# A graph layer with 27 instead of 35 ranges summed through slots, and the other nodes by row gathers

## The chip, the cores and the metric

The kernel runs on one core of one Trainium2 chip. The metric is the device time of one execution in microseconds; the time of a kernel is the median of its runs. TensorE multiplies matrices and writes to PSUM, VectorE (DVE in the profile) and ScalarE (ACT) compute on SBUF and PSUM, GpSimd (POOL) issues the gathers, and SyncE (SP) issues most of the plain transfers. Each engine works through its own queue in order.

## The reference

A graph has 6250 nodes with 128 features each and 100000 edges (src, dst, type), sorted by dst. Every edge sends the source's row, multiplied by one of two weight matrices, to its destination; the messages are summed per destination, the node's own product is added, and a ReLU, a residual and a layer norm follow.

```python
Xs = X[src]
m_data = Xs @ W_data.T + b_data
m_ctrl = Xs @ W_control.T + b_control
msg = jnp.where((edge_types == 0)[:, None], m_data, m_ctrl)
agg = jax.ops.segment_sum(msg, dst, num_segments=X.shape[0])
out = agg + (X @ W_self.T + b_self)
x = _layernorm(x + jax.nn.relu(out), axis=-1)
```

## The kernel before

**The message table.** For 49 blocks of 128 nodes both products with bias are made (line 448 and 450), split into three bf16 parts whose sum is the float32 value, and kept in SBUF as `m3` (98 tiles of 128 rows by 384 columns: a block and a type each). The same goes to DRAM as `table` (line 479), from which rows can be gathered. `brows` holds the three bf16 parts of the bias as rows, and the product with `one3` (line 450) adds it; the parts are made on VectorE (lines 399 to 408).

**Ranges with slots.** The first 35 x 160 = 5600 nodes are 35 ranges of `WN` = 160 destinations, in groups of 1, 2 and eight times 4. The edges of a range (at most 21 x 128) are loaded as `win`. `ranks` (from line 589) numbers the edges of each of the 98 tiles of `m3`: for each of 21 steps VectorE makes a mask of the tile numbers (`hots`, line 645), TensorE counts with it in PSUM (`rk`, line 655), and VectorE reads the count off with a maximum (`slot`, line 659). An edge thus has a tile and a slot, 32 per tile. Masks `hr` and `two` (674, 680) and the product `vt` (689) put each edge's row and destination into its slot; the rows go to DRAM as `packed` and come back to all partitions as `rows` (line 840, 784 KB for a range). Edges without a slot go into a list of up to 64 per range (`hl`, line 756), whose rows are gathered from `table` in pairs of ranges (`sr`, line 797, index `at`, line 785).

`sums` then works through the 25 groups of four tiles of each range. VectorE turns `rows` into a mask (line 847) and makes the mask of destinations `hot2` (line 854). TensorE picks the rows out (`g`, line 867), ScalarE writes them to SBUF as `gs` (line 413), and TensorE adds them to the destinations (`a`, lines 881 and 884).

**Gathered nodes.** The last 650 nodes are six blocks of up to 128 (`gathered`, from line 899). A block has up to 18 tiles of 128 edges. For each tile GpSimd issues a gather of 128 rows of `table`, 768 bytes each (`t_msg`, line 931, four buffers), VectorE makes a mask of destinations (`t_hot`, line 936, three buffers), and TensorE adds the rows to `ga` (line 942). That is 93 tiles.

**Closing.** `close` adds the three parts on VectorE (line 530), adds the residual, and normalises (lines 538 to 576), for the ranges of a group or for a gathered block. `counts` collects how many edges were summed; if they aren't all, a slower path would run, which isn't the case here.

**The order.** All operations are recorded with a cost and a due time, and `Plan.run` puts them into one order: for each engine the operation that can start first, the earliest due first. The engines' queues, and which of ScalarE and VectorE takes a copy, come from this list. `T0` and `TW` are the due time of the first range and the step from range to range in this plan; `gathered` spreads its tiles evenly from `g0` to `g1`. A wait between engines costs the plan `SEM`; a transfer's time is its `lat`. A buffer that is used again makes its next user wait for all users of the one before.

Of the kernel before, what the change touches and what calls it, by code (L numbers as in the profile page):

```python
# [10 lines left out]
F32 = mybir.dt.float32  # L11
BF16 = mybir.dt.bfloat16
I32 = mybir.dt.int32
AF = mybir.ActivationFunctionType
ALU = mybir.AluOpType
AX = mybir.AxisListType
SP = mybir.EngineType.SP
# [4 lines left out]
P = 128  # L22
D = 128
D3 = 3 * D
# [9 lines left out]
WIN = KT * P  # L34
GROUPS = [1, 2] + [4] * 8
NW = sum(GROUPS)
# [194 lines left out]
def sums_over_windows(ctx, tc, x, xt, edges, w, bias, out, total):  # L231
# [16 lines left out]
    def C(shape, dtype, name):  # L248
        return Buf(plan, const, shape, dtype, name, 1)

    T0 = 46.0
    TW = 13.0
# [5 lines left out]
        r0.t, edges.rearrange("(p h k) c -> p h (k c)", p=125, h=RH)[:, :, 1:2]), 0.0, w=[r0],  # L258
        lat=2.0)
    w_sb = C([D, D3], F32, "w_sb")  # L260
    b3 = C([3, D3], F32, "b3")
    add("ACT", 0.1, lambda: A.dma_start(w_sb.t, w), 0.0, [], [w_sb], lat=2.5)
    add("ACT", 0.1, lambda: A.dma_start(b3.t, bias.to_broadcast([3, D3])), 0.0, [], [b3], lat=2.5)

# [7 lines left out]
    def vec(due, cols, fn, r, w, rate=1.04):  # L272
        return add("DVE", dve(cols, rate), fn, due, r, w)
# [68 lines left out]
    def count_rows():  # L342
# [13 lines left out]
        in_offset=bass.IndirectOffsetOnAxis(ap=row_i.t[:, 0:1], axis=0)),  # L356
        0.5, [row_i], [er], lat=2.5)
    dst_f = C([NBD, RL], F32, "dst_f")
# [19 lines left out]
    def load_edges(b, n, out_, due, buf, key, engine):  # L378
        def fn():
# [6 lines left out]
            else:  # L386
# [4 lines left out]

    part = C([3, D3], BF16, "part")
    left = C([3, D3], F32, "left")
    acc3 = C([3, D3], F32, "acc3")
    part2 = C([3, D3], BF16, "part2")
    brows = C([P, D3], BF16, "brows")
    bd = 2.0
    vec(1, D3, lambda: V.memset(brows.t, 0.0), [], [brows], 0.3)
    vec(bd, D3, lambda: V.tensor_copy(part.t, b3.t), [b3], [part])
    vec(bd, D3, lambda: V.tensor_scalar_mul(acc3.t, part.t, ident.t[:3, 0:1]),  # L400
        [part, ident], [acc3])
    vec(bd, D3, lambda: V.tensor_sub(left.t, b3.t, part.t), [b3, part], [left])
    vec(bd, D3, lambda: V.tensor_copy(part2.t, left.t), [left], [part2])
    vec(bd, D3, lambda: V.scalar_tensor_tensor(acc3.t, part2.t, ident.t[:3, 1:2], acc3.t,
                                               op0=ALU.mult, op1=ALU.add),
        [part2, ident, acc3], [acc3])
    vec(bd, D3, lambda: V.tensor_sub(left.t, left.t, part2.t), [part2, left], [left])
    vec(bd, D3, lambda: V.scalar_tensor_tensor(brows.t[:3, :], left.t, ident.t[:3, 2:3], acc3.t,
                                               op0=ALU.mult, op1=ALU.add),
        [left, ident, acc3], [brows])  # L410

# [18 lines left out]
    for q in range(NS):  # L430
# [12 lines left out]

        def products(bs=bs, c=c, xa=xa, mp=mp, q=q):
            for i, b in enumerate(bs):
                o = mp.t[:, 256 * i : 256 * i + 256]
                at = (b - c * CH) * P
                T.matmul(o, xa.t[:, at : at + P], w_sb.t[:, : 2 * D], start=i == 0, stop=False,  # L448
                         skip_group_check=True)
                T.matmul(o, one3.t, brows.t[:, : 2 * D], start=False, stop=q < DQ,  # L450
                         skip_group_check=True)
        add("PE", 0.55 * nb, products, due, [xa, w_sb, one3, brows], [mp])
        ts = slice(4 * q, 4 * q + 2 * nb)
# [445 lines left out]
    def gathered(bi, when, step):  # L899
# [28 lines left out]
        for k in range(nt):  # L928
            at = when + step * k
            m = B(work, [P, D3], BF16, "t_msg", 4)  # L930
            add("POOL", 1.25, lambda m=m, k=k: G.indirect_dma_start(  # L931
                out=m.t, out_offset=None, in_=table[:, :],
                in_offset=bass.IndirectOffsetOnAxis(ap=idx.t[:, k : k + 1], axis=0)),
                at, [idx, table_b], [m], lat=2.0)
            hot = B(work, [P, P], BF16, "t_hot", 3)
            vec(at + 2, P, lambda hot=hot, k=k: V.tensor_scalar(
                hot.t, iota1_b.t[:, :P], code.t[:, k : k + 1], None, op0=ALU.is_equal),
                [code, (iota1_b, 0)], [hot], 0.26)

            def mm(m=m, hot=hot, k=k):  # L940
                for j in range(-(-nn // R)):
                    T.matmul(ga.t[R * j : R * j + R, :D3], hot.t[:, R * j : R * j + R], m.t,  # L942
                             start=k == 0, stop=False, skip_group_check=True)
            add("PE", 0.165, mm, at + 4.5, [hot, m], [ga])
# [8 lines left out]
    for gi, nw in enumerate(GROUPS):  # L953
        if gi == 0:
            when, step, engines = 4.0, 0.5, ["SP"]
        elif gi == 1:
            when, step, engines = 19.0, 0.9, ["SP", "ACT"]
        else:
            when, step, engines = T0 + w0 * TW - 58, 1.8, ["SP"]
            if gi == 2:  # L960
                when, step = 40.0, 1.3
        todo.append((gi, w0, nw, when, step, engines))
        w0 += nw
# [8 lines left out]
    total_tiles = sum(GT)  # L972
    g0, g1 = T0 + 2.5 * TW, T0 + (NW - 2.5) * TW
    done = 0
# [151 lines left out]
```

## Time and profile before

| what | us |
|---|---|
| median of 3 runs | 669.11 (669.08 to 672.03) |
| profiled execution | 620.9 |
| its span, first to last instruction | 619.1 |
| VectorE: counts of line 659, 128x392, 168 times | 93.7 |
| VectorE: masks of line 854, 175 times | 93.6 |
| VectorE: masks of line 847, 70 times | 43.0 |
| ScalarE: `gs`, 836 times | 353.8 |
| TensorE: `g`, line 867, 3430 times | 316.8 |
| TensorE: `a`, line 881, 3360 times | 306.0 |
| TensorE: `ga`, line 942, 363 times | 39.0 |
| GpSimd: `t_msg`, 93 times | 95.5 |

The times per group are busy times; products of TensorE that run beside each other on different columns of the array overlap, so the rows of TensorE add up to more than its busy time. In the same way an instruction of VectorE can begin before the one ahead of it has ended. The profiled execution is shorter than the median of the runs; comparisons within the profile use its own time.

The transfers, by their queue, are packets, megabytes and share of the 16 engines' time:

```profile
q1 hardware_dynamic: 45585, 48.25, 24.3%
q0 software_dynamic: 5664, 10.97, 6.7%
q10 hardware_dynamic: 7494, 6.53, 3.4%
```

Queue 0 is GpSimd's, with 93 row gathers, 18 list gathers and one of edges; queue 1 is SP's and queue 10 ScalarE's.

### The profile page before, as it was taken

Reading aid. Unit: us, or ns where it says so; the run is one execution under the profiler, and the core shown is the slowest. Engines: PE = TensorE matmul, PEld = TensorE weight load, DVE = VectorE, ACT = ScalarE, POOL = GpSimd, SP = SyncE. Lnnn points to the kernel's source line nnn. Section 1 sums busy time; section 2 is a strip of 40 time slices with the busy share of each in tenths; the row PEclk is TensorE's granted clock in tenths of the full one; section 3 lists DMA queues with packets and bytes.
Section 4 is the critical chain, followed back from the end, with each engine's and each line's share of the span. In section 5 each row is a group of like instructions: output and inputs, shape, how many; then the busy total and the mean of one; then the engine's idle time right before and its main releaser. Section 6 shows DMA issues by size and latency. Waiting matters only on the chain.

```text
span 619.1 us, 31669 instructions
## 1 busy us (share of the span) xinstructions
PE 540.9 (87%) x13418; PEld 415.5 (67%) x13418; DVE 521.1 (84%) x1846; ACT 445.7 (72%) x1153; POOL 115.1 (19%) x119
## 2 busy tenths in 40 slices
PE   3899959979998898989979998998899889998991
PEld 2555637757776677767767877777777678776670
DVE  4899789989999899988998999899988987866602
ACT  1477736757677767867867788778777777788991
POOL 1000230020421034310134410045100333110000
PEclk9999988989999999999999999999999999999997
DMA  4688651063135223540344143315420443043001
GB/s 113 194 269 266 196 178 38 25 207 104 44 103 153 84 65 100 177 127 5 118 141 140 51 134 99 101 50 168 133 85 4 156 122 109 24 139 105 27 4 28
DMA packets 58893, 67.85 MB, mean 110 GB/s; under 512 B 19707, under 2 KB 49906, under 8 KB 58743
## 3 DMA queue, kind: packets, MB, share of 16 engines
q1 hardware_dynamic: 45585, 48.25, 24.3%
q0 software_dynamic: 5664, 10.97, 6.7%
q10 hardware_dynamic: 7494, 6.53, 3.4%
q8 instruction: 107, 1.75, 1.1%
q14 instruction: 43, 0.35, 0.2%
HBM read 50.72 MB, written 13.27 MB: 103 GB/s over the span
## 4 chain that ended last, share of the span: by engine, by line
DVE 55%; PE 30%; ACT 5%; DMA 4%; issue 4%; SPq 1%; POOL 0%; ACTq 0%; DVEq 0%
DVE hot L854 10%; DVE slot L659 9%; PE a L881 9%; PE g L867 8%; DVE hots L645 4%; PE rk L655 4%; DVE rows L847 4%; DVE two L680 4%; ACT gs L413 3%; PE g L448 3%; DVE s L530 3%; DVE st L542 2%; DVE hr L674 2%; DVE xr L538 2%; PE a L884 2%
## 5 line engine op out<-in xcount | busy, mean ns | idle before, releaser
L413 ACT CAST gs<-g 128x384 bf16<-128x384 f32 x836 | 353.8, 481 | 93.5 <-PE g L867 88.6
L867 PE MATMUL g<-m,rows 128*32 128x384 bf16 x3430 | 316.8, 329 | 1.9 <-issue 1.1
L881 PE MATMUL a<-gs,hot 128*32 128x384 bf16 x3360 | 306.0, 331 | 9.1 <-ACT gs L413 5.1
L867 PEld LDWEIGHTS <-rows 128*32 128x32 bf16 x3430 | 217.4, 135 | 14.6 <-issue 2.1
L884 PE MATMUL a<-gs,hot 128*32 128x128 bf16 x2520 | 200.9, 220 | 0.1
L881 PEld LDWEIGHTS <-hot 128*32 128x32 bf16 x3500 | 153.4, 95 | 62.8 <-issue 27.0
L931 POOL DMA_INDIRECT t_msg<-table,t_idx x93 | 95.5, 1027 | 243.3 <-PE ga L942 196.9
L659 DVE TENSOR_REDUCE slot<-rk 128x4 f32<-128x392 f32 (+2 forms) x210 | 106.6, 507 | 18.2 <-PE rk L655 15.5
L854 DVE TENSOR_TENSOR hot<-iota_b,to_d 128x800 bf16<-128x800 bf16 x175 | 93.6, 565 | 21.0 <-PE a L884 16.6
L884 PEld LDWEIGHTS <-hot 128*32 128x32 bf16 x2625 | 98.0, 96 | 4.7 <-issue 0.3
L655 PE MATMUL rk<-hots,rest 128*32 128x392 bf16 (+2 forms) x800 | 73.2, 317 | 25.9 <-DVE slot L659 25.2
L655 PE MATMUL rk<-hots,tri 128*32 128x392 bf16 (+2 forms) x840 | 82.7, 314 | 0.0
L655 PEld LDWEIGHTS <-rest 128*32 128x32 bf16 x800 | 34.9, 96 | 48.4 <-issue 43.6
L645 DVE TENSOR_TENSOR hots<-iota_b,st 128x392 bf16<-128x392 bf16 (+2 forms) x210 | 60.1, 327 | 1.8 <-PE vt L689 1.6
L797 POOL DMA_INDIRECT sr<-table,at x18 | 17.1, 949 | 183.4 <-DVE at L785 99.9
L847 DVE TENSOR_SCALAR rows<-rows,pid 128x1568 bf16<-128x1568 bf16 x70 | 43.0, 635 | 0.0
L942 PE MATMUL ga<-t_msg,t_hot 128*32 128x384 bf16 x363 | 39.0, 326 | 2.7 <-DVE s L530 2.2
L655 PEld LDWEIGHTS <-tri 128*32 128x32 bf16 x840 | 36.3, 97 | 3.5 <-issue 0.3
L530 DVE TENSOR_TENSOR s<-s,a 128x128 f32<-128x128 f32 x70 | 19.8, 284 | 18.0 <-ACT s L527 16.8
L448 PE MATMUL g<-w_sb,xc 128*128 128x256 f32 x98 | 32.8, 430 | 1.3 <-PE rk L655 0.9
L689 PEld LDWEIGHTS <-two 128*64 128x64 bf16 x735 | 18.6, 108 | 16.7 <-DVE two L680 13.7
L689 PE MATMUL vt<-hots,two 128*64 128x98 bf16 x735 | 24.1, 208 | 6.0 <-DVE two L680 5.7
(174 smaller groups left out, 568.7 us busy)
## 6 DMA issues: line engine op xcount, KB each, us to landing
rows<-packed SPq DMA_DIRECT2D x35, 784.0 KB
table<-m SPq DMA_DIRECT2D x12, 384.0 KB
table<-m ACTq DMA_DIRECT2D x12, 384.0 KB
xc<-in_xt SPq DMA_DIRECT2D x8, 320.0 KB
xr<-in_x SPq DMA_DIRECT2D x8, 256.0 KB
out<-xr SPq DMA_DIRECT2D x8, 256.0 KB
gl<-sr SPq DMA_DIRECT2D x35, 48.0 KB
xc<-in_xt ACTq DMA_DIRECT2D x6, 256.0 KB
```

The source lines that it names most:

```text
L413: [("ACT", act(cols), lambda: A.copy(o(), src())), ("DVE", dve(cols), lambda: V.tensor_copy(o(), src()))], None, None, due, r, w, lat)
L448: T.matmul(o, xa.t[:, at : at + P], w_sb.t[:, : 2 * D], start=i == 0, stop=False, skip_group_check=True)
L645: vec(due - (2.0 if k else 0.5), nw * NT, lambda k=k, hot=hot, k0=k0: V.tensor_tensor(hot.t[:, k - k0].rearrange("p w (c d) -> p w c d", d=2),
L655: T.matmul(acc.t[R * j : R * j + R, : nw * NT], wt.t[:, R * j : R * j + R], m, start=start, stop=stop, skip_group_check=True)
L659: vec(due, nw * NT, lambda k=k: V.tensor_reduce(slot.t[:, k, :], acc.t[:, : nw * NT].rearrange("p (w c) -> p w c", c=NT), axis=AX.X, op=AL ...
L689: T.matmul(vv()[q : q + 64, i // 2, :], two.t[:, (k - k0) * nw + i].rearrange("p f r -> p (f r)"), hot.t[:, k - k0, i, :], start=k == 0 an ...
L847: add("DVE", dve(half * NT, 0.26), lambda sp=sp, rs=rs: V.tensor_scalar(sp.t[:, rs], sp.t[:, rs], pid1.t, None, op0=ALU.is_equal), due - 4 ...
L854: V.tensor_tensor(hot2.t[:, c0 : c0 + 5].rearrange("p g (c d) -> p g c d", d=2), iota1_b.t.rearrange("p (c d) -> p c d", d=2)[:, None].to_ ...
L867: T.matmul(gp.t[R * t : R * t + R, :D3], sp.t[:, :, 4 * g + t], m3.t[:, 4 * g + t, :], start=True, stop=True)
L881: T.matmul(a.t[R * j : R * j + R, :D3], hot2.t[:, g, R * j : R * j + R], gs.t, start=g == 0, stop=False, skip_group_check=True)
L884: T.matmul(a.t[R * c : R * c + R, D3:], hot2.t[:, g, P:], gs.t[:, c * D : (c + 1) * D], start=False, stop=last, skip_group_check=True)
L931: add("POOL", 1.25, lambda m=m, k=k: G.indirect_dma_start(out=m.t, out_offset=None, in_=table[:, :], in_offset=bass.IndirectOffsetOnAxis(a ...
```

## The change

Two of the eight groups of four ranges go: 27 ranges (4320 nodes) are summed through slots, and the last 1930 nodes are 16 blocks with 273 gathers. Gathered rows have eight buffers instead of four, their masks four instead of three. The bias is split on ScalarE and VectorE as one row, and its three parts are put into `brows` by three transfers. The plan gets other due times and other costs: the first range is due at 36 instead of 46, the first two groups' ranking has its own starts and steps, the loads of `r0` and `er` are costed longer, and the products of the message table are planned one block at a time instead of two. Gathers are spread from two ranges after the first to two before the last, instead of two and a half. From about line 410 on, a line of the kernel after stands seven lines above its place before.

```diff
-GROUPS = [1, 2] + [4] * 8
+GROUPS = [1, 2] + [4] * 6
...
-    T0 = 46.0
+    T0 = 36.0
...
-        lat=2.0)
+        lat=4.5)
...
-    b3 = C([3, D3], F32, "b3")
+    b1 = C([1, D3], F32, "b1")
...
-        0.5, [row_i], [er], lat=2.5)
+        0.5, [row_i], [er], lat=6.5)
...
-    vec(bd, D3, lambda: V.tensor_copy(part.t, b3.t), [b3], [part])
-    vec(bd, D3, lambda: V.tensor_scalar_mul(acc3.t, part.t, ident.t[:3, 0:1]),
-        [part, ident], [acc3])
...
+    vec(0.2, D3, lambda: V.memset(brows.t, 0.0), [], [brows], 0.3)
+    add("ACT", 0.4, lambda: A.copy(bparts[0].t, b1.t), 1, [b1], [bparts[0]])
+    vec(1, D3, lambda: V.tensor_sub(left.t, b1.t, bparts[0].t), [b1, bparts[0]], [left])
+    add("ACT", 0.4, lambda: A.copy(bparts[1].t, left.t), 1, [left], [bparts[1]])
+    vec(1, D3, lambda: V.tensor_sub(bparts[2].t, left.t, bparts[1].t), [left, bparts[1]],
+        [bparts[2]])
+    for i in range(3):
+        add("SP", 0.1, lambda i=i: S.dma_start(brows.t[i : i + 1, :], bparts[i].t), 1.5,
+            [bparts[i]], [(brows, i)], lat=2.0)
...
-        def products(bs=bs, c=c, xa=xa, mp=mp, q=q):
-            for i, b in enumerate(bs):
+        for i, b in enumerate(bs):
+            def product(i=i, b=b, c=c, xa=xa, mp=mp, q=q):
...
-        add("PE", 0.55 * nb, products, due, [xa, w_sb, one3, brows], [mp])
+            add("PE", 0.58, product, due, [xa, w_sb, one3, brows], [mp])
...
-            m = B(work, [P, D3], BF16, "t_msg", 4)
+            m = B(work, [P, D3], BF16, "t_msg", 8)
...
-            hot = B(work, [P, P], BF16, "t_hot", 3)
+            hot = B(work, [P, P], BF16, "t_hot", 4)
...
-            when, step, engines = 4.0, 0.5, ["SP"]
+            when, step, engines = 3.0, 0.9, ["SP"]
         elif gi == 1:
-            when, step, engines = 19.0, 0.9, ["SP", "ACT"]
+            when, step, engines = 18.0, 1.1, ["SP", "ACT"]
         else:
             when, step, engines = T0 + w0 * TW - 58, 1.8, ["SP"]
             if gi == 2:
-                when, step = 40.0, 1.3
+                when, step = 36.0, 1.3
...
-    g0, g1 = T0 + 2.5 * TW, T0 + (NW - 2.5) * TW
+    g0, g1 = T0 + 2 * TW, T0 + (NW - 2) * TW
```

More of the change, by code (lines that the diff above doesn't have):

```diff
@@ L258, in sums_over_windows @@
         r0.t, edges.rearrange("(p h k) c -> p h (k c)", p=125, h=RH)[:, :, 1:2]), 0.0, w=[r0],
-        lat=2.0)
+        lat=4.5)
     w_sb = C([D, D3], F32, "w_sb")
-    b3 = C([3, D3], F32, "b3")
+    b1 = C([1, D3], F32, "b1")
     add("ACT", 0.1, lambda: A.dma_start(w_sb.t, w), 0.0, [], [w_sb], lat=2.5)
-    add("ACT", 0.1, lambda: A.dma_start(b3.t, bias.to_broadcast([3, D3])), 0.0, [], [b3], lat=2.5)
+    add("ACT", 0.1, lambda: A.dma_start(b1.t, bias), 0.0, [], [b1], lat=2.5)
     iota_f = C([P, P], F32, "iota_f")
@@ L389, in load_edges @@
         add(engine, 1.0 if b else 0.1, fn, due, [first] if b else [], [(buf, key)], lat=2.0)
[L392 to L395, printed above, removed]
+    left = C([1, D3], F32, "left")
+    bparts = [C([1, D3], BF16, f"bpart{i}") for i in range(3)]
     brows = C([P, D3], BF16, "brows")
-    bd = 2.0
-    vec(1, D3, lambda: V.memset(brows.t, 0.0), [], [brows], 0.3)
-    vec(bd, D3, lambda: V.tensor_copy(part.t, b3.t), [b3], [part])
-    vec(bd, D3, lambda: V.tensor_scalar_mul(acc3.t, part.t, ident.t[:3, 0:1]),
-        [part, ident], [acc3])
[L402 to L410, printed above, removed]
+    vec(0.2, D3, lambda: V.memset(brows.t, 0.0), [], [brows], 0.3)
[7 more added lines that the diff above has]
+            [bparts[i]], [(brows, i)], lat=2.0)
     evict = lambda o, src, cols, due, r, w, lat=0.0: add(
```

## The prediction, made before the run

> **What bounds the kernel now.** I read the page's busy shares first, then the slices, then the chain of waits for landmarks, then a table of stretches, then GpSimd's own timeline.
>
> ```profile
> span 619.1 us, 31669 instructions
> PE 540.9 (87%) x13418; PEld 415.5 (67%) x13418; DVE 521.1 (84%) x1846; ACT 445.7 (72%) x1153; POOL 115.1 (19%) x119
> DVE  4899789989999899988998999899988987866602
> DVE 55%; PE 30%; ACT 5%; DMA 4%; issue 4%; SPq 1%; POOL 0%; ACTq 0%; DVEq 0%
> ```
>
> VectorE and TensorE are both near full, and VectorE carries 55% of the chain that ends last. Its row of slices is at 8 to 9 until the last tenth of the span and then falls: three regimes. The chain shows where they meet, because each group of four ranges builds one list (`hl`, line 756) at the end of its ranking:
>
> ```profile
> 126.58 0.96 DVE hl L756
> ...
> 244.12 0.97 DVE hl L756
> ...
> 483.00 0.96 DVE hl L756
> 544.01 0.56 PE vt L775 x24
> ```
>
> Columns: start, length, what. The third group's list is at 126.6; from 244.1 to 483.0 four groups pass, 59.7 us each; the last group's list is at 544, and 75 us of ranges without any ranking follow. In stretches:
>
> ```profile
> core 0: us, PE busy (x) PEld busy (x) DVE busy (x) ACT busy (x) POOL busy (x), PEclk, DMA share, GB/s
> 220.00:500.00 280.00, 256.89 (x6939) 205.53 (x6933) 257.39 (x878) 214.96 (x568) 70.06 (x69) 1.00 0.34 103
> 545.00:605.00 60.00, 54.69 (x1457) 41.71 (x1451) 28.07 (x94) 53.44 (x143) 1.90 (x2) 1.00 0.20 69
> ```
>
> In the middle VectorE is busy 257.4/280 = 92%, so 54.9 us per group; TensorE shows the same 92%. At the end VectorE is at 47% and TensorE and ScalarE lead. GpSimd has 70 us of work in 280.
>
> **What the Trainium skill says.** "Perfetto Trace Analysis", section "Identifying the Most-Contended Engine": occupancy is a fair measure for VectorE, matmul occupancy isn't, because matmuls are pipelined, and weight-load share is better. Here weight loads are 205.5/280 = 73%, so I take VectorE as the bound of the middle and TensorE's 92% as overstated. The same page, "DMA Instruction — SWDGE (GPSIMD)": the profiler ends a gather when its descriptors are written, not when the data is there. The trace agrees: the first row gather takes 0.96 us on GpSimd, yet TensorE waits until 4.74 us after its start. "SBUF — State Buffer", section "SBUF: two separate sides": a VectorE instruction in a two-port fast mode and GpSimd's descriptor writing lock each other out. The trace shows at most a mild form:
>
> ```profile
> L931 POOL DMA_INDIRECT t_msg<-table,t_idx x93: 940/946/2396, 74.4 to 528.1; - x93
> ...
> L936 DVE TENSOR_SCALAR t_hot<-iota_b,t_code x93: 235/247/487, 44.5 to 529.7; 128x128 bf16<-128x128 bf16 x93
> ```
>
> Minimum, median, maximum in ns: half of the gathers are within 6 ns of the fastest although VectorE is 92% busy around them.
>
> **The change, part by part.**
>
> *Eight ranges leave (two groups of four).* Count times mean over the VectorE rows of the groups table gives about 616 us against 521 busy, since neighbours overlap a little: I scale sums by 521/616 = 0.85. With the instruction counts of both programs' issue order: ranking falls from 316 to 248, slot and hot masks (lines 847, 854) from 143 to 111, closing from 72 to 56, small copies by 3, the bias by 3: 121 less, 103 scaled. ScalarE's evictions fall from 836 to 647 of the 128x384 kind, 189 x 0.48 = 91 us by the mean. TensorE: a unit of one `g` and one `a` product takes 0.37 to 0.41 us where TensorE streams (534 matmuls, 11 to a unit, in the stretch 580 to 600), so eight ranges of 25 are 80 us, with their ranking about 100.
>
> *180 more row gathers (93 to 273), ten more blocks (6 to 16).* VectorE pays one `t_hot` a gather, 0.258 us, and per block: two adds 0.55, relu-add 0.29, statistics 0.29 and 0.18, seven small operations 1.1, half of the normalising 0.2, nine list instructions 1.48: 4.1 us, or 0.23 per gather at about 17.5 gathers. So 180 x 0.49 = 88, scaled 75. TensorE: four matmuls of 384 columns, side by side, 0.165 us a gather where they stream: 30 us, and 5 for ten blocks' own product. ScalarE: 10 us.
>
> Net: VectorE 521 - 103 + 75 = 493, priced instruction by instruction 577 x 0.85 = 488. TensorE loses about 65, ScalarE about 80. So the time saved is far from eight ranges' 2 x 59.7 = 119.
>
> *Where it falls.* Counting gather matmuls between one range's products and the next in the issue order: before, 42 gathers in the four groups of the middle, 10.5 a group; after, 223 in ranges 2 to 21, 44.6 a group, and 42 more in the ranges after the last ranking. A group after: 54.9 + 34.1 x 0.49 x 0.85 = 69.1 us of VectorE. TensorE and ScalarE now have slack (TensorE 256.9/280 x 59.7 = 54.8, and 34 x 0.165 + 1 more: 61; ScalarE 45.8 and 2 more: 48), so VectorE's share should rise from 92% to 94 or 95%: 73 us. The ends: at 92%, 75; at 97%, 71.
>
> *GpSimd's pace.* Gathers can't follow each other faster than this:
>
> ```profile
> 224.72 0.95 POOL L931 DMA_INDIRECT t_msg<-table,t_idx  x1 [0.30 <-issue]
> 225.97 0.95 POOL L931 DMA_INDIRECT t_msg<-table,t_idx  x1 [0.30 <-PE ga L942]
> ```
>
> 1.25 us each with 0.30 between. A group needs 44.6 + 2 for its long lists (line 797): 58 us of 73. It fits with 20% to spare, but GpSimd's queue is in order: a list gather that waits for VectorE's `at` (line 785; 99.9 us of such waits before, in eight waits) holds all row gathers behind it, and TensorE, in order too, then stops at a `ga` product. Eight buffers instead of four are what covers this: at one product per 1.6 us they hold 13 us. I cost it at 1 us a group inside the 73; from below it is nothing, and if the cover is gone, 5 to 10 a group. Row gathers move 98 KB each, and queue 0 took 6.7% of the engines for 111: 287 would be about 19%, beside 20 to 25% of the rest. No bound.
>
> *Buffers and loads.* Four `t_hot` instead of three, and the separate product of each block with its own issue slot: nothing. Ten more loads of edges, rows and results on SP: 0.4 us of issue each, behind which nothing is late; at worst 4 us.
>
> *The start.* The bias leaves VectorE (eight instructions, 3.4 us, until 10.25) for a chain of ScalarE and VectorE copies and three transfers. In SP's queue these stand behind some 20 loads, whose issues ended at 11.2 before, so `brows` comes at about 13 to 14, not 10.25. Ahead of it TensorE does the first range's ranking, which started at 10.3 and can now start at 4 to 5, when its edges have landed. VectorE has 107 us of work in the first 127 either way. I take 4 us gained, between 10 gained and 4 lost.
>
> *The end.* Five ranges without ranking follow as before, but now with 42 gathers: TensorE, near full there, pays 42 x 0.165 + 1.4 = 8 us, plus a block to close: 9 (5 to 20).
>
> **Sum.** 122.6 + 5 x 73 - 5 (the first such group took 54.7 where the others took 60) + 75.2 + 9 = 567 us of span against 619.1. The profiled execution as a whole took 620.9, the median of the runs shown is 669.11, so 48 us lie outside what this profile explains. If they scale (a slower clock outside the profiler would do that; no row shows it), 669.11 x 567/619.1 = 613; if they are fixed, 617. VectorE-bound work scales less than TensorE's with TensorE's clock, which pulls down. I take 613.
>
> **Rivals.** (a) *Gathers set the pace without undoing the gain:* TensorE stops at `ga` products and groups take 79 to 83 us. For it: in-order queues, 80% use of GpSimd. Against: 0.5 us of such waits in the whole profile before. Span 597, so 645. (b) *Slower:* one mechanism, the cycle of a gather (buffer free, issue, landing, product) is stretched by VectorE's lock on the port and by the broadcast `rows` transfers. It decides when a cycle exceeds 83.5/46.6 = 1.79 us: 122.6 + 5 x 84 - 5 + 75.2 + 9 = 622, already above 619.1, or 672. For it: the 2.4 us maximum; against: the median. (c) *Faster than forecast:* the 48 us are TensorE's clock, and the lighter TensorE gets most of it back: the 567 us then carry some 25, so 592. (d) *The sums cancel:* VectorE's 488 to 493 plus more stops leave it at 619.
>
> **How the numbers follow.** Forecast 0.62 (595 to 632 alone), (a) 0.16, (b) 0.10, (c) 0.09, (d) 0.03. Below half a per cent a difference can't be told in this kernel. Faster 0.62 + 0.16 + 0.09 = 0.87, same 0.03, slower 0.10. The range takes in most of (a) and (c): 588 to 648.
>
> **What would show it.** Right: lists (line 749 after) 70 to 76 us apart, VectorE over 92% busy between them, GpSimd at 70 to 80% of its pace, almost no wait of TensorE or GpSimd on a landing, span 550 to 585. Wrong: TensorE idle before `ga` on a DMA or VectorE waiting for `t_hot` buffers (a, b); gathers with a median far over 0.95 us (b); a start later than 127; the timed median not following the span.

## The result, and the profile after

The changed kernel takes 703.86 us (median of 4 runs, 700.36 to 706.68) beside 669.13 for the kernel before (669.08 to 672.03): ratio 1.0498, 95% interval [1.0466, 1.053]. It is slower; the forecast was 613 us. Its page:

```profile
span 698.7 us, 27684 instructions
...
PE 533.3 (76%) x11386; PEld 369.0 (53%) x11386; DVE 490.3 (70%) x1905; ACT 375.5 (54%) x953; POOL 294.2 (42%) x295
...
DVE  5798368987877378878588775977866768664432
...
PE 56%; DVE 9%; ACT 9%; issue 9%; another core or an unknown queue 6%; DMA 1%; ACTq 0%; DVEq 0%; SPq 0%
```

The work is what was forecast: VectorE's 490.3 us lie inside the 488 to 493 of the prediction. But VectorE is now busy 70% of the span instead of 84%, its slices stand at 7 and 8, and it carries 9% of the chain instead of 55%. No engine is full. So the time is in waits. The waits by engine and line (total us, how often, the longest):

```profile
PEld L874 <- issue: 156.5, 227, 5.2
ACT gs L406 <- PE g L860: 125.9, 167, 9.2
...
PE a L874 <- ACT gs L406: 59.9, 80, 5.2
ACT gs L406 <- remote: 52.7, 15, 7.5
```

All are on the path `g` product, eviction `gs`, `a` product. None of them names a gather, and in the whole list no engine waits for the landing of gathered rows: that is not what is late. "issue" is time for which the profile shows no reason, "remote" a releaser that it doesn't show. One stop, in the timeline (start, length, what, idle time before and its releaser):

```profile
230.33 0.95 POOL L924 DMA_INDIRECT t_msg<-table,t_idx  x1 [0.30 <-issue]
...
231.58 0.95 POOL L924 DMA_INDIRECT t_msg<-table,t_idx  x1 [0.30 <-issue]
...
231.68 0.48 PE L860 MATMUL g<-m,rows 128*32 128x384 bf16 x1 [0.34 <-issue]
...
232.40 0.10 PEld L874 LDWEIGHTS <-hot 128*32 128x32 bf16 x1 [1.29 <-issue]
...
232.83 0.95 POOL L924 DMA_INDIRECT t_msg<-table,t_idx  x1 [0.30 <-issue]
...
234.08 0.94 POOL L924 DMA_INDIRECT t_msg<-table,t_idx  x1 [0.30 <-issue]
...
236.80 1.24 ACT L406 CAST gs<-g 128x384 bf16<-128x384 f32 x3 [7.52 <-remote]
...
237.33 0.51 PE L874 MATMUL a<-gs,hot 128*32 128x384 bf16 x4 [5.17 <-ACT gs L406]
```

GpSimd writes one gather after another from 225.1 to 235.0. The last `g` product starts at 231.68; ScalarE, idle, evicts at 236.80, and then three evictions at once. TensorE's wait is put down to ScalarE, but ScalarE only sat there. What came late is TensorE's report that the products were done: the trace records no step of TensorE's semaphore (the counter on which the other engines wait) between 229.47 and 236.72, then three within 0.23 us (worked out from the trace, in which some 2% of these records are missing). The ends of matmuls in these profiles are modelled, so a product that ended late can't be told from a signal that left late; below, "TensorE's signals are late" means either. The stretch with the stop, and the one behind it (columns as in the table of stretches above: start and end, length, busy us of each engine, TensorE's granted clock, share of the transfers, GB/s):

```profile
225.00:246.00 21.00, 12.31 (x220) 8.16 (x210) 9.67 (x37) 7.19 (x19) 10.05 (x10) 0.76 0.36 114
246.00:254.00 8.00, 6.61 (x183) 5.13 (x182) 6.70 (x23) 5.66 (x17) 3.15 (x3) 1.00 0.55 181
```

The clock is 0.76 over this stretch and back at 1.00 after it. The Trainium skill, "TensorE: Matmul & The Clock Gate", section "HAM oscillation — how this bites in real kernels", says that gaps of over about 3.4 us without matmuls make the clock fall. In this trace less is enough: the clock is recorded at half from 231.6 to 241.8, so its fall comes as the 5 us stop begins, not after it, and in the 3.4 us before each of the trace's eleven falls 8 to 51 matmuls started, with no pause between starts over 2.7 us (worked out from the trace; where work streams, as in e7 below, 3.4 us hold about 79). Over the whole span the clock is 0.932, against 0.982 in the profile before.

One number in all this can't be understood without the next: the profiled execution of the kernel before took 620.9 us, all its timed runs here 669. The experiments show that these are two conditions, and that the prediction was worked out in the one and measured in the other.

### The profile page after: what moved, and what is told of

It is laid out like the page before. It is cut to its first block, busy times and chain, and to the rows that moved or that the text cites. A ratio compares the mean times of both kernels' runs of the same rounds, so it can differ in the third digit from the quotient of the medians.

```text
span 698.7 us, 27684 instructions
## 1 busy us (share of the span) xinstructions
PE 533.3 (76%) x11386; PEld 369.0 (53%) x11386; DVE 490.3 (70%) x1905; ACT 375.5 (54%) x953; POOL 294.2 (42%) x295
## 4 chain that ended last, share of the span: by engine, by line
PE 56%; DVE 9%; ACT 9%; issue 9%; another core or an unknown queue 6%; DMA 1%; ACTq 0%; DVEq 0%; SPq 0%
PE a L874 18%; PE g L860 17%; PE ga L935 8%; ACT gs L406 8%; PE rk L648 5%; PE a L877 3%; PE vt L682 2%; DVE slot L652 2%; DMA rows<-packed 1%; DVE rows L840 1%; DVE s L523 1%; PE a L480 1%; DVE two L673 1%; DVE hot L847 1%
## 5 line engine op out<-in xcount | busy, mean ns | idle before, releaser
L406 ACT CAST gs<-g 128x384 bf16<-128x384 f32 x647 | 284.4, 482 | 251.3 <-PE g L860 125.9
L924 POOL DMA_INDIRECT t_msg<-table,t_idx x273 | 278.1, 1019 | 270.6 <-PE g L860 106.2
L874 PE MATMUL a<-gs,hot 128*32 128x384 bf16 x2592 | 252.6, 344 | 98.3 <-ACT gs L406 59.9
L860 PE MATMUL g<-m,rows 128*32 128x384 bf16 x2646 | 263.5, 344 | 8.3 <-issue 6.9
L874 PEld LDWEIGHTS <-hot 128*32 128x32 bf16 x2700 | 124.2, 98 | 179.0 <-issue 156.5
L860 PEld LDWEIGHTS <-rows 128*32 128x32 bf16 x2646 | 157.9, 136 | 25.7 <-issue 13.3
L877 PE MATMUL a<-gs,hot 128*32 128x128 bf16 x1944 | 162.2, 226 | 3.7 <-issue 3.7
L929 DVE TENSOR_SCALAR t_hot<-iota_b,t_code 128x128 bf16<-128x128 bf16 x273 | 69.1, 258 | 102.9 <-PE g L860 46.6
L935 PE MATMUL ga<-t_msg,t_hot 128*32 128x384 bf16 x1083 | 111.9, 334 | 5.5 <-issue 3.1
L877 PEld LDWEIGHTS <-hot 128*32 128x32 bf16 x2025 | 78.2, 99 | 14.3 <-issue 9.2
L935 PEld LDWEIGHTS <-t_hot 128*32 128x32 bf16 x1083 | 47.4, 98 | 15.9 <-issue 6.6
```

What stands on the lines that cost most here:

```text
L406: [("ACT", act(cols), lambda: A.copy(o(), src())), ("DVE", dve(cols), lambda: V.tensor_copy(o(), src()))], None, None, due, r, w, lat)
L860: T.matmul(gp.t[R * t : R * t + R, :D3], sp.t[:, :, 4 * g + t], m3.t[:, 4 * g + t, :], start=True, stop=True)
L874: T.matmul(a.t[R * j : R * j + R, :D3], hot2.t[:, g, R * j : R * j + R], gs.t, start=g == 0, stop=False, skip_group_check=True)
L877: T.matmul(a.t[R * c : R * c + R, D3:], hot2.t[:, g, P:], gs.t[:, c * D : (c + 1) * D], start=False, stop=last, skip_group_check=True)
L924: add("POOL", 1.25, lambda m=m, k=k: G.indirect_dma_start(out=m.t, out_offset=None, in_=table[:, :], in_offset=bass.IndirectOffsetOnAxis(a ...
L929: vec(at + 2, P, lambda hot=hot, k=k: V.tensor_scalar(hot.t, iota1_b.t[:, :P], code.t[:, k : k + 1], None, op0=ALU.is_equal), [code, (iota ...
```

## The experiments

Each batch of runs ran on one chip, beside its own runs of the kernel before. These came out at two values, with nothing in between:

| batch | runs | chip, by its number in the results | kernel before, median and extremes |
|---|---|---|---|
| first | e0 to e3 | 7 | 670.33 (668.31 to 673.07), 18 runs |
| second | e4 to e7 | 3 | 624.75 (622.62 to 626.91), 7 runs |
| third | e8 to e11 | 7 | 669.66 (665.75 to 671.93), 23 runs |
| fourth | e12 to e15 | 4 | 668.82 (667.81 to 671.63), 8 runs |
| fifth | e16, e17 | 4 | 625.15 (621.45 to 626.93), 7 runs |

I call them the 669 and the 625 condition. The number of the chip doesn't settle which comes (number 4 had both), and what sets it stays open. The runs for the result are in the 669 condition, the profile before in the 625 condition. Ratios are to the kernel before in the same batch, with 95% intervals.

### First batch (669): halves of the change, and the gathers taken out

**e0, the kernel before again.**

> The kernel before, unchanged, for a second profile. If its one profile (span 619) was an unusual execution and the usual one has stops of TensorE as the changed kernel shows them, its span comes out near 667 with TensorE idle over 90 us and its clock halved for 50 us or more. If the 48 us between the profile and the timed runs lie outside the kernel, the span is again near 619 with a granted clock of 0.98. Timed ratio 1.00 in both.

669.69 us, ratio 0.9997 [0.9981, 1.0013]. Its profile is worth more than its time, since it is the same program as in the profile before, 48.5 us longer (span 667.6 against 619.1). First the wait list of the profile before, then of e0:

```profile
ACT gs L413 <- PE g L867: 88.6, 135, 8.6
...
PEld L881 <- issue: 27.0, 82, 1.4
```

```profile
ACT gs L413 <- PE g L867: 112.5, 149, 7.4
...
PEld L881 <- issue: 76.1, 151, 2.0
```

The wait of the weight loads of `a` rises by 49 us (waits overlap, so they don't add up to the span): the 48 us "outside what this profile explains" are the same waits on the path `g`, `gs`, `a`. TensorE's clock isn't what makes them: it is at half for 38.0 us here (50 or more were expected) and 24.9 us in the profile before, and 13 us more at half speed hold at most 7 us. If all gathers of GpSimd share the difference, 93 of rows, 18 of lists and one of edges, it is 48.5/112 = 0.43 us each; if the row gathers alone carry it, 0.52. This run alone doesn't show that it is the gathers; the next ones do.

**e1, everything but the fewer ranges; e2, only the fewer ranges.**

```diff
e1, against the kernel after:
-GROUPS = [1, 2] + [4] * 6
+GROUPS = [1, 2] + [4] * 8
e2, against the kernel before:
-GROUPS = [1, 2] + [4] * 8
+GROUPS = [1, 2] + [4] * 6
```

> All edits of the change but the one to the groups: 35 ranges and 93 gathers as before. If the loss comes from the gathers, this is within 1% of before. If the lead-in, the later bias rows, the plan's due times or the buffers carry it, it is 2 to 5% slower.

> The kernel before with two groups of four ranges fewer and nothing else: 273 gathers through four row buffers and three mask buffers. If the gathers carry the loss, this is at least as slow as the change, 700 us or more, and slower still (720 to 760) if the ring of buffers sets their pace. If the other edits carry it, near 620.

e1: 677.19 us, 1.0079 [1.0054, 1.0104]. e2: 686.03 us, 1.0223 [1.0183, 1.0263], less than the 700 or more that I had expected. The exchange of ranges for gathers alone makes it slower by 16 us, and the rest alone by 7. "The rest" hides two effects of opposite sign, as e11 below shows: it differs from e2 only by the bias rows and the plan and takes 668.27 us, 18 less, while the step from its four buffers to eight costs 22.

**e3, no row gathers.** The products read a constant tile.

```diff
-            m = B(work, [P, D3], BF16, "t_msg", 8)
-            add("POOL", 1.25, lambda m=m, k=k: G.indirect_dma_start(
...
+            add("PE", 0.165, mm, at + 4.5, [hot, fixed], [ga])
```

> The changed kernel without its row gathers: TensorE's 1083 products for the gathered nodes read one constant tile, so the gathered nodes' sums are left out; masks and products stay. If engine work sets the time, it stays near 695 to 705. If the gathers (their pace, landings or waits) set it, it falls to the sum of the engines' work, about 570 to 610.

555.28 us, 0.8278 [0.8254, 0.8301], even less than the 570 to 610 that I had expected. All products, masks and blocks are still there: the 273 gathers hold 149 us of the 704 of the result, or 135 of the 690 that the same kernel takes in e8.

### Second batch (625): which part of a gather costs

**e4, gathers issued, nobody reads them** (the products read the constant tile). **e5, plain loads** by SyncE in the gathers' place. **e6, GpSimd busy** with an iota in place of each gather. **e7, four buffers.**

```diff
e5:
-            add("POOL", 1.25, lambda m=m, k=k: G.indirect_dma_start(
-                out=m.t, out_offset=None, in_=table[:, :],
-                in_offset=bass.IndirectOffsetOnAxis(ap=idx.t[:, k : k + 1], axis=0)),
+            add("SP", 0.4, lambda m=m, k=k: S.dma_start(
+                m.t, table[(4 * k + bi) * P : (4 * k + bi) * P + P, :]),
e7:
-            m = B(work, [P, D3], BF16, "t_msg", 8)
+            m = B(work, [P, D3], BF16, "t_msg", 4)
...
-            hot = B(work, [P, P], BF16, "t_hot", 4)
+            hot = B(work, [P, P], BF16, "t_hot", 3)
```

> The changed kernel with all 273 gathers issued as before, but TensorE's products for the gathered nodes read one constant tile, so no engine waits for a gathered row and those nodes' sums are left out. If a gather costs because GpSimd's work on it (0.95 us each) delays what TensorE reports to the other engines, whoever reads the rows, this stays at 670 to 705. If the cost is the wait for landings and for free row buffers between GpSimd and TensorE, it falls to 555 to 590, near the run without gathers.

> The changed kernel with each gather replaced by a plain load of 128 rows of the same table, 98 KB, issued by SP into the same eight buffers and read by the same products; the rows aren't those of the edges, so the gathered nodes' sums are left out. If GpSimd's part of a gather is the cost: 555 to 585. If moving and landing the 27 MB, or the ring of buffers, is the cost: 670 to 700.

> The changed kernel with each gather replaced by an iota of 512 numbers on GpSimd, about as long as a gather's 0.95 us and without a transfer; products read a constant tile, so the gathered nodes' sums are left out. If any work of GpSimd delays the others: 670 to 705. If only the writing of transfer descriptors does: 553 to 570.

> The changed kernel with four row buffers and three mask buffers, as before. If gathers set in long rows of up to eight are what stops TensorE for 5 us and more and halves its clock, shorter rows help: 685 to 697. If the eight buffers are cover against landings, it is slower than the change: 710 to 740.

e4: 563.97 us, 0.9014 [0.8976, 0.9052]. e5: 560.09, 0.8988 [0.8933, 0.9042]. e7: 569.65, 0.9055 [0.8995, 0.9114]. In this condition the changed kernel with four buffers is 9% faster than before, and a gather costs (569.65 - 560.09)/273 = 0.04 us. Neither expectation for e7 had that, since both took the 669 condition for granted. e6 came to 687.05 and tells nothing of the question: without buffers that come free one by one, the planner put the gathered work elsewhere, and GpSimd waited 263 us for list indices from VectorE. e12 puts it better.

e7's waits, in the lines that answer to those of the kernel after:

```profile
ACT gs L406 <- PE g L860: 101.6, 147, 8.4
...
PEld L874 <- issue: 29.9, 78, 1.8
...
PE a L874 <- ACT gs L406: 9.8, 17, 1.7
```

29.9 us where the kernel after has 156.5. Yet GpSimd writes its gathers just as fast in both; the first line below is the kernel after, the second (in its own fence) e7; minimum, median and maximum in ns:

```profile
L924 POOL DMA_INDIRECT t_msg<-table,t_idx x273: 940/946/1728, 77.3 to 666.5; - x137
```

```profile
L924 POOL DMA_INDIRECT t_msg<-table,t_idx x273: 940/947/2025, 79.2 to 545.9; - x137
```

So GpSimd's row doesn't tell the conditions apart. TensorE's signal does. For every `gs` that found ScalarE idle for 0.15 us or more (264 in the kernel after, 165 in e7) I take the time from the start of the last `g` product that signals to its eviction, sorted by the share of this time in which GpSimd was writing a gather (worked out from the traces; median us, from the quarter with the least writing to that with the most):

```
kernel after (669)   0.54  0.78  1.26  0.93
e7 (625)             0.48  0.49  0.54  0.49
```

### Third batch (669): the same kernels again

> The changed kernel unaltered, to see whether its 704 us belongs to the kernel or to the executions in which the kernel before takes 669 us. Theory (a TensorE result is seen late by the other engines while GpSimd writes the addresses of a gather, and only in some executions): if the kernel before takes about 670 us beside it, 700 to 706 us again (ratio 1.05); if the kernel before takes about 625 us beside it, 560 to 575 us (ratio 0.90 to 0.92), which is what the forecast's span of 567 us would give. Rival (the changed kernel is slower in itself): ratio 1.05 in either case.

> The changed kernel with each row gather replaced by a plain load of the same 98 KB, issued by SyncE. It leaves out the gathered nodes' true sums. Theory (GpSimd's writing of addresses is the cost, not the bytes and not the readers): 555 to 570 us whether the kernel before takes 670 or 625 us beside it. Rival (the bytes of the gathers or the buffers they come into are the cost): 690 to 705 us where the kernel before takes 670 us.

> The changed kernel with all 273 gathers issued, but their products reading a constant tile, so that no instruction of TensorE waits for a gather. It leaves out the gathered nodes' true sums. Theory: where the kernel before takes 670 us beside it, 680 to 705 us (the addresses are still written); where it takes 625 us, 560 to 575 us. Rival (late landing of the gathered rows is what TensorE waits for): 550 to 575 us in both cases.

> The changed kernel with 4 buffers for gathered rows in place of 8, and 3 for the comparisons in place of 4. Theory: the buffers have little part in it, so within 2 per cent of the changed kernel beside it: about 690 to 710 us where the kernel before takes 670 us, 560 to 575 us where it takes 625 us. Rival (eight buffers let gathers run in long unbroken trains on GpSimd, and these are the harm): where the kernel before takes 670 us, 670 us or less, clearly under the changed kernel beside it.

The edits are those above (e8 the changed kernel, e9 as e5, e10 as e4, e11 as e7).

| kernel | 625 condition | 669 condition |
|---|---|---|
| changed kernel | not run | 690.21, 1.0311 [1.0264, 1.0358] |
| plain loads | 560.09 | 560.94, 0.8371 [0.8333, 0.8408] |
| nobody reads | 563.97 | 905.36, 1.3511 [1.3437, 1.3584] |
| four buffers | 569.65 | 668.27, 0.9981 [0.9963, 0.9999] |

The changed kernel is slower than before again, but by 3.1% where it was 5.0%, and under the 700 to 706 us expected: the two values aren't the whole story, and what makes the difference of 14 us between two batches of one condition isn't known. Plain loads of the same bytes into the same buffers take 560 to 561 us in both: neither bytes nor buffers nor readers carry the condition. With the gathers unread, so that no product of TensorE waits for one, I expected 680 to 705 us and got 905. And four buffers turned out 22 us better than eight, as the rival to my theory had it: long trains are the harm. A train is here a row of gathers, those of lists included, less than 0.6 us apart. Both results point the same way. Stretches of e10 (columns as above), in and after a train of 31 gathers:

```profile
660.00:677.00 17.00, 11.57 (x264) 8.26 (x263) 12.28 (x47) 8.76 (x22) 8.36 (x7) 0.90 0.49 149
677.00:697.00 20.00, 5.71 (x41) 2.05 (x41) 1.50 (x7) 1.02 (x3) 15.19 (x16) 0.54 0.29 77
...
718.00:735.00 17.00, 15.22 (x405) 11.52 (x396) 15.48 (x58) 11.02 (x30) 1.19 (x2) 1.00 0.31 92
```

41 matmuls in 20 us of GpSimd's writing, 405 in 17 us almost without it. A stretch of e4, the same program in the 625 condition, inside a train of 48:

```profile
350.00:382.00 32.00, 29.64 (x779) 23.29 (x775) 31.03 (x125) 22.23 (x58) 24.76 (x24) 1.00 0.53 156
```

779 matmuls under the same writing. And the end of e10's train in the timeline:

```profile
700.00 0.95 POOL L927 DMA_INDIRECT t_msg<-table,t_idx  x1 [0.30 <-issue]
700.49 0.48 PE L648 MATMUL rk<-hots,rest 128*32 128x392 bf16 x1 [1.62 <-issue]
701.25 0.95 POOL L927 DMA_INDIRECT t_msg<-table,t_idx  x1 [0.30 <-issue]
701.90 0.10 PEld L648 LDWEIGHTS <-rest 128*32 128x32 bf16 x1 [2.01 <-issue]
...
703.29 0.49 PE L648 MATMUL rk<-hots,rest 128*32 128x392 bf16 x1 [2.32 <-issue]
...
704.69 0.10 PEld L874 LDWEIGHTS <-hot 128*32 128x32 bf16 x1 [2.69 <-issue]
...
706.26 0.95 POOL L927 DMA_INDIRECT t_msg<-table,t_idx  x1 [0.30 <-issue]
711.79 1.24 ACT L406 CAST gs<-g 128x384 bf16<-128x384 f32 x3 [25.44 <-remote]
```

TensorE starts single instructions 1.41, 1.39 and 1.40 us apart, with no wait shown, and the eviction is released 4.6 us after the train's end, when ScalarE has stood idle for 25 us. The longer GpSimd writes without a pause, the slower it gets. Matmuls started per us, by time since the beginning of a train, in trains of five gathers or more (worked out from the traces; e8 has only six of these):

```
us into the train      0-2.5  2.5-5  5-7.5  7.5-10  later
e10, nobody reads (669)  14.0   6.0    4.5    3.2    1.5 (10 to 20), 0.9 (from 20)
e8, kernel after (669)   13.3   3.6    3.7    1.7
e4, nobody reads (625)   19.0  18.7   21.8   22.9   20 to 26
e7, four buffers (625)   25.7  25.0   23.3   24.8   20 to 26
```

This accounts for the buffers. Most trains are short with eight and with four (1.5 and 1.4 gathers on average), but with eight they grow up to 9, with four up to 5. More than 2.5 us into a train, e8 spends 60.6 us and starts 434 matmuls, e11 43.9 us and 624; at the 23.3 per us of e7 that is 42 and 17 us lost, an estimate whose difference of 25 us is near the 22 measured. Unread, trains have 14.4 gathers on average. A gather costs (668.3 - 565.2)/273 = 0.38 us with four buffers (against e12 below, another batch), (690.2 - 560.9)/273 = 0.47 with eight, and (905.4 - 560.9)/273 = 1.26 unread: as long as GpSimd takes for it with its 0.30 us pause.

### Fourth batch (669): busy without addresses, distance, dose

**e12, GpSimd sets each buffer to zero instead of gathering** (four buffers): every wait and the order stay.

```diff
-            add("POOL", 1.25, lambda m=m, k=k: G.indirect_dma_start(
-                out=m.t, out_offset=None, in_=table[:, :],
-                in_offset=bass.IndirectOffsetOnAxis(ap=idx.t[:, k : k + 1], axis=0)),
+            add("POOL", 1.25, lambda m=m: G.memset(m.t, 0.0),
```

> The changed kernel with 4 buffers for gathered rows, and each row gather replaced by GpSimd setting the same buffer to zero, which the product then reads: GpSimd's part in the order of the work and every wait stay, but no addresses are written and nothing is transferred. It leaves out the gathered nodes' sums. Theory (the writing of a gather's addresses delays TensorE's signals): 555 to 575 us whether the kernel before takes 670 or 625 us beside it. Rival (products that wait for an instruction of GpSimd are the cost, whatever it does): where the kernel before takes 670 us, 655 to 670 us, as with the gathers.

565.19 us, 0.8457 [0.8429, 0.8485]. That products wait for GpSimd is not the cost. The chain of this run looks as the forecast had it, VectorE first:

```profile
DVE 65%; PE 17%; issue 3%; ACT 2%; DMA 2%; another core or an unknown queue 0%; ACTq 0%; DVEq 0%; SPq 0%
```

The memset takes 433 ns, less than a gather's 946, so GpSimd is busy for less than half as long; this run alone doesn't exclude that a longer instruction of another kind would cost too.

**e13, the second step planned later** (four buffers).

```diff
-                add("PE", 0.22, stage2, d + 0.9, [gs, (hot2, g // 5)], [a])
+                add("PE", 0.22, stage2, d + 1.45, [gs, (hot2, g // 5)], [a])
```

> The changed kernel with 4 buffers for gathered rows, and the second step of each range's sums planned about one step later behind its eviction, so that one more independent step of TensorE lies between. Theory, first form (each signal of TensorE comes 0.8 us late while addresses are written, a fixed delay that more work in between covers): where the kernel before takes 670 us, 635 to 655 us. Theory, second form (signals are held back and come out at a limited rate, which no distance covers): 660 to 672 us, as without the edit. Where the kernel before takes 625 us, 560 to 575 us for both.

664.72 us, 0.9937 [0.9913, 0.9962], 0.5% under e11 of the batch before. That is where the second form had it: one more step in between covers next to nothing.

**e14, 31 ranges and 183 gathers** (four buffers).

```diff
-GROUPS = [1, 2] + [4] * 6
+GROUPS = [1, 2] + [4] * 7
```

> The changed kernel with 4 buffers for gathered rows and 31 ranges instead of 27, so that about 180 gathers are left of 273. If each gather costs about 0.43 us where the kernel before takes 670 us, 90 gathers fewer give back 39 us and four ranges more cost some 35 to 50 us of engine work: 660 to 680 us, nearly the same as with 27 or 35 ranges. If the gathers cost less than that, 680 to 700 us; if more, under 655 us. Where the kernel before takes 625 us: 590 to 605 us.

677.97 us, 1.0128 [1.0089, 1.0166], 10 us over e11: four ranges cost what 90 gathers give back and 10 us more. That lies where 0.43 us a gather had it, but what a range costs in this condition wasn't measured apart.

**e15, the kernel before with each row gather issued twice.**

```diff
+            sp2 = B(work, [P, D3], BF16, "t_again", 2)
+            add("POOL", 1.25, lambda m=sp2, k=k: G.indirect_dma_start(
+                out=m.t, out_offset=None, in_=table[:, :],
+                in_offset=bass.IndirectOffsetOnAxis(ap=idx.t[:, k : k + 1], axis=0)),
+                at, [idx, table_b], [sp2], lat=2.0)
```

> The kernel before with each of its 93 row gathers issued a second time, into a spare buffer that nobody reads. Theory: where the kernel before takes 670 us, 93 more times 0.43 us, 40 us longer: 700 to 720 us. Where it takes 625 us: 620 to 635 us. Rival (a gather costs only through the instructions that wait for its rows): 665 to 680 us where the kernel before takes 670 us.

761.05 us, 1.1408 [1.1337, 1.148]. 93 gathers that nobody reads cost 92 us, 0.99 each. The sign was expected, the size, 40 us, was far too small. The pairs make longer trains than e0 has (1.9 gathers on average and up to 13, against 1.4 and up to 5), which goes the way of e10; whether that makes the whole 92 us wasn't shown.

### Fifth batch (625): away from gathers, and shorter trains

```diff
e16, four buffers:
-GROUPS = [1, 2] + [4] * 6
+GROUPS = [1, 2] + [4] * 9
e17, as e13:
-            m = B(work, [P, D3], BF16, "t_msg", 4)
+            m = B(work, [P, D3], BF16, "t_msg", 2)
```

> The changed kernel with 39 ranges instead of 27 (and 4 buffers), so that 3 row gathers are left of 273: the opposite move. VectorE's work per range follows from the kernels at hand: 35 ranges with 93 gathers keep it busy 523 us, 27 ranges with 273 gathers 490 us, so with 0.256 us for each comparison a range is worth (523 - 490 + 180 x 0.256) / 8 = 9.9 us, and 39 ranges come to 523 + 4 x 9.9 - 90 x 0.256 = 540 us. Theory (the gathers alone make the difference between 561 and 704 us): with VectorE 87 to 90 per cent busy, as in the run with the memsets, 600 to 625 us, wherever it runs. Rival (more ranges cost as much as the gathers they save, as the 31 ranges suggest): 665 to 700 us where the kernel before takes 670 us.

> The changed kernel with only 2 buffers for gathered rows and the second step planned later, so that GpSimd can write no long train of gathers. If trains are what makes a gather dear (1.26 us each in trains of 14, 0.38 us each in trains of 1.4): 640 to 662 us where the kernel before takes 670 us. If two buffers make TensorE wait for the landing instead: 665 to 720 us. Where the kernel before takes 625 us: 570 to 640 us.

Both ran in the 625 condition, so neither answers what it was made for. e16: 659.44 us, 1.0559 [1.0526, 1.0593], above the 600 to 625 that I expected:

```profile
PE 578.5 (88%) x14434; PEld 440.4 (67%) x14434; DVE 538.2 (82%) x1806; ACT 487.9 (75%) x1259; POOL 23.9 (4%) x31
```

VectorE's sum was right (540 forecast, 538.2), but not that it would be 87 to 90% busy: TensorE now shares the bound. With 3 row gathers left, 24 of GpSimd in all, an estimate for the 669 condition is 659 us if lists cost nothing and 670 at 0.43 us each; so whether it would be under the kernel before there is open, and it was not run. e17: 769.67 us, 1.231 [1.2259, 1.2362], far above the 570 to 640 expected in this condition. In its list of waits:

```profile
PE ga L935 <- DMA t_msg<-table,t_idx: 114.2, 93, 3.6
```

Two buffers make TensorE wait for the landings, and so show the other limit: short trains alone don't make a kernel fast.

### A version for both conditions

Of the changed kernels that compute the whole result, only the one with four buffers (e7, e11) was measured in both: 0.9055 and 0.9981 of the kernel before. With the second step later (e13) it is 0.6% [0.4, 0.9] faster than the kernel before in the 669 condition. None was found that gains much there.

## Why the prediction was wrong

**The step that failed** is in its sum: "48 us lie outside what this profile explains. If they scale (a slower clock outside the profiler would do that; no row shows it), 669.11 x 567/619.1 = 613; if they are fixed, 617." They were neither. They go with GpSimd's gathers, 0.43 us each for 112 (e0), and the change makes 288 of these. The sum priced a gather at 0.258 us of VectorE and 0.165 of TensorE, and what its writing does to TensorE's signals at nothing. With this one term, 567 + 2 around the span + 288 x 0.43 = 693, between the 690 and 704 measured. That it lands so near is in part luck: the price isn't fixed (0.38 to 1.26 us, with the length of the trains), and counted for row gathers alone, 273 x 0.52, the sum is 711. The two numbers that the prediction could see, a profile of 620.9 and three runs at 669.11, were a sign that the profile was of another condition; I treated the difference as a factor, without asking which count in the kernel 48 us could follow.

**What held, in the condition of the profile.** e7 is the change with four buffers, and its median of 569.65 us is the forecast span and the 2 around it. Its lists, in the chain (start, length, what):

```profile
191.30 0.97 DVE hl L749
...
262.94 0.96 DVE hl L749
...
407.44 0.96 DVE hl L749
...
481.08 0.97 DVE hl L749
```

From 191.3 to 481.1 four groups pass, 72.4 us each; the forecast was 73. The last list was forecast at 122.6 + 5 x 73 - 5 = 482.6 and came at 481.1; the span was forecast at 567 and is 569.2. TensorE's busy time falls from 540.9 to 474.9 (66; forecast about 65), ScalarE's from 445.7 to 367.6 (78; about 80). VectorE's share in the middle, over the same stretch in the kernel after and in e7:

```profile
100.00:500.00 400.00, 311.73 (x6991) 216.97 (x6990) 308.32 (x1142) 209.55 (x546) 190.36 (x187) 0.93 0.36 105
```

```profile
100.00:500.00 400.00, 349.74 (x9106) 272.02 (x9096) 372.00 (x1431) 268.20 (x698) 249.61 (x243) 0.99 0.46 132
```

372/400 = 93% in e7 (94 to 95% forecast), 77% in the kernel after. There the lists of the full groups are 89 us apart at the end (from 505.95 to the last at 594.6).

**What held in neither.** "I take 4 us gained" at the start: the three transfers of the bias rows come so late that TensorE stands, as the kernel after shows:

```profile
PEld L443 <- DMA brows<-bpart: 7.8, 1, 7.8
```

e7 has 8.1 us of it, and its third list comes at 131, not 122.6. The next list follows 60 us later (191.3), not 68, and the end took 88 us instead of 84 (the 75.2 us in the sum count from the product at 544.0; from the last list itself, at 542.65, they are 76.5). So the steady groups were forecast rightly, but that the last list and the span of e7 fit within 2 us is luck: a late start, a quick first group and a longer end cancel.

**Rivals.** (a) expected stops at `ga` products: 5.5 us of idle time stand before them in the kernel after. (b) had the sign, not the size (672), and the wrong mechanism: VectorE doesn't stretch the gathers (median 946 ns as before); GpSimd's gathers hold TensorE's signals back. "Eight buffers instead of four are what covers this" was wrong in sign in the 669 condition: they let trains grow (22 us worse), and in the 625 condition four suffice. (c) took the 48 us for TensorE's clock. The clock is low here too, at half for 97 us of the kernel after and for 34 us of e7, where work has already thinned out; these 63 us at half speed hold at most 31 of the 129 us between the two spans. (d) had more stops cancel the gain; in the 669 condition they cost more than the gain, in the 625 condition the gain stayed.

**Open.** What sets the condition; and by which way GpSimd's writing holds TensorE back. Plain loads differ from gathers both in who writes the addresses and in the queue that carries them. The evictions of the kernel after speak for the writing: with GpSimd writing less than a tenth of the time, the median is 0.54 us without packets of its queue under way (52 evictions) and 0.59 with them (14); with GpSimd writing over three tenths of it, 0.86 (71) and 1.37 (95). But no run separates the two. Late instructions for TensorE are a rival that no run excludes either; against it, the trace of e10 has no packet of the two instruction queues under way between 674 and 711 us, while TensorE starts single instructions. The changed kernel itself, with eight buffers, never ran in the 625 condition.

## What to carry to other kernels

When the profiled execution and the timed runs of one kernel differ by more than their spread, the difference is a term of the sum: ask which count it follows (here GpSimd's gathers) before scaling it. A wait that names an idle engine points past it, to a signal that came late; sort the delays by what other engines did at the moment, since the engine that costs the time may have an unchanged row of its own. Measure a kernel with many gathers in more than one batch beside its rival, and keep the trains of gathers short, as far as their readers don't have to wait for landings.

## What the runs showed of the hardware

- In the 669 condition TensorE starts fewer and fewer instructions while GpSimd writes gathers without a pause: 14.0 matmuls per us in the first 2.5 us, 0.9 after 20 us (e10). In the 625 condition, with the same program, 19 to 26 throughout (e4).
- Of the signals between the computing engines, those from TensorE are late (kernel after; medians without and with GpSimd writing): from the end of a product to ScalarE's start 0.19 and 0.51 us, to VectorE's 0.11 and 0.53. From ScalarE to the product that waits for it 0.05 us in both, from VectorE 0.06 and 0.05.
- TensorE's clock fell to half without a pause of 3.4 us before: in the kernel after 8 to 51 matmuls had started in the 3.4 us before each fall.
- GpSimd's memsets slow VectorE's masks, its gathers don't: `t_hot` takes 398 ns on average where a memset overlaps it and 248 where none does (e12); 256 and 250 ns with and without a gather beside it (e11).
